# The first expert layer: routing by two tiles inside the last feed, experts in written order, fetched rows added tile by tile in the next layer

## The chip, the core and the metric

The kernel runs on one core of one Trainium2 chip. The metric is the device time of one execution, in microseconds (us), as the median of several runs. One core has five engines that work beside each other: TensorE (PE; its weight loads are listed apart as PEld), VectorE (DVE), ScalarE (ACT), GpSimd (POOL) and SyncE (SP). In this kernel SP issues nearly all DMAs, ACT some, and POOL those that take their row numbers from a tile (indirect DMAs: scatters and gathers).

## The reference, cut to what matters

The program is a stack of four layers of cross attention, self attention and feed-forward on 16 x 64 = 1024 tokens of width 256. The change touches the end of the first self-attention stage, the first feed-forward stage and the opening of the next cross attention.

The first self attention is a four-layer encoder with linear attention. Of each of its layers only the second half matters here, `x + relu(layernorm(x) @ W1 + b1) @ W2 + b2` with 1024 hidden features, and then a last layer norm, whose scaled result is added to the tokens. The expert layer after it is

```
logits = x @ gate_w.T
probs = softmax(logits)
top2_w, top2_idx = top_k(probs, 2)
cap = int(1.25 * T / E)                      # 160 of T = 1024, E = 8
counts = bincount(top2_idx.reshape(-1), length=E)
keep = (counts <= cap)
comb = zeros((T, E)).at[arange(T)[:, None], top2_idx].add(top2_w) * keep[None, :]
h = relu(einsum('th,ehf->tef', x, W1) + b1)
y = einsum('teh,ehf->tef', h, W2) + b2
out = einsum('te,tef->tf', comb, y)
```

so that an expert that more than 160 tokens choose gives nothing at all. In the program its output is added to the tokens. The next cross attention normalises the tokens, forms scores of the 64 slots of each of 16 groups against 1601 context rows, takes the softmax over the slots, and feeds weighted context sums to a recurrent cell (GRU), three times over.

## The kernel before, in words

**Tiles and stages.** The tokens lie in `self.x` as NT = 8 tiles of P = 128 tokens by D = 256 features (KC = 2 blocks of 128). `STAGES` (L2590) runs eleven stages one after the other, among them `l0_attn`, `l0_ffn` and `l1_xattn`. Where a stage sets `self.pinned`, TensorE takes its matmuls in the order in which they are written; engines wrapped in `Written` (L51, whose calls are all recorded as L59) keep their written order likewise. Elsewhere the scheduler orders.

**l0_attn** works on two halves, a and b, of HT = 4 tiles. Each half's work is written as generators, and `go(generator, n)` advances one by n steps, so the code writes out by hand how the halves take turns. The half-layer above is `feed` (L635): two steps that transpose the normalised tokens into hT (`turn`), eight steps c0 to c7 of one 128-feature group each (matmuls named lin_t, then a relu on ACT or DVE into h1T), four steps t0 to t3 of one tile each (matmuls named lin, added to y), and `finish` (L664) for each pair of tiles: the normalisation n and, in the last feed, its scale and the addition into x. `measure` takes a pair's mean and variance, `norm` makes n. In each step `squares` (L441) lets ACT do some of the squares of context rows ("junk" in the profile) which later stages need; the calls of one feed sum to 26.

After the layer loop comes, in this order (L822-L832): the rest of a's last feed; `squares(999)`, all squares left over, at once; b's last feed, into whose later steps the routing of a is put; the routing of b.

**Routing.** `route(s)` (L695) does four tiles at a time: normalise, transpose, 16 gate matmuls, then on DVE logits, a comparison of each expert's logit with each other's (rk_gt, rk_eq, of 4 x 8 x 8 columns), their sum rank, and sel (rank under 2). Two to five matmuls named pos count, for each token, how many tokens before it chose each expert; the count of half a is kept for half b. From pos come place, whether it fits within the 160 places, and two row numbers for each token: put, where its row is written, and get, where its result will be. Eight indirect DMAs on POOL (L758) scatter the rows of n into the DRAM buffer `taken`, which holds 160 places for each expert and spare rows behind.

**l0_ffn** (L850) loads `taken` back: xs holds the first 128 places of all experts (four DMAs), xw the last 32 (four DMAs, in groups of 32 partitions). All are transposed on TensorE into xsT. Then the softmax of the logits, and the weight wt of each token and choice. For each expert come the loads of W1 and W2 (SP's queue), eight matmuls (hidden), relu (hT), four matmuls (out), the bias into ys, and a DMA of ys into the DRAM buffer `given`; after every fourth expert 16 matmuls do the last 32 places of four experts, into yw and again into `given`. This stage isn't pinned. At its end (L941-L947) 16 indirect DMAs on POOL gather two rows for each token out of `given` into `got`, each followed by a DVE operation that multiplies by wt and adds to x.

**l1_xattn** (L950) loads keys (cT) and rows (cn) of two groups for each tile, and two small tiles raw and raw2 of GRU biases. `product(mqk)` multiplies two weights together, `first(tile)` normalises a tile into s, `queries` makes pq and qT. `biases` (L1012) splits raw into three bfloat16 parts by ten DVE operations on 32 partitions. `attend` makes scores (sc, TensorE), takes them off (ACT), transposes them (turn) and softmaxes over slots (DVE, POOL); `product(mvg)` multiplies two more weights; `update` sums context rows (pu, 52 matmuls) and runs the GRU. The order is that of L1270 onwards: mqk, first(tiles[0]), its queries, load_rows of tile 0, keys of tile 1, load_rows of tile 1, biases, attend, product(mvg), then the loop over tiles and iterations.

Of the kernel before, what the change touches and what calls it, by code (L numbers as in the profile page):

```python
# [20 lines left out]
P = 128  # L21
# [5 lines left out]
NCH = 13  # L27
# [37 lines left out]
class Sections:  # L65
# [343 lines left out]
    def l0_attn(self):  # L409
# [5 lines left out]
        self.route = to = Streamed(0)  # L415
        for name, shape, dt in (("logits", [P, NT, E], F32), ("count", [P, 2, E], F32), ("hot", [P, NT, 2, E], F32),
                                ("put", [P, NT, 2], I32), ("get", [P, NT, 2], I32)):
            setattr(to, name, pool.tile(shape, dt, tag=name, name=name))
# [12 lines left out]
            self.taken[: E * CAP].rearrange("(j p) d -> p j d", p=P), zero.unsqueeze(1).to_broadcast([P, E * CAP // P, D]))  # L431
        views = dram_disjoint_views(self.taken, 2 * NT)
        with ExitStack() as ctx:
# [201 lines left out]
            def feed(s, w, last=False):  # L635
# [15 lines left out]
                for t in range(HT):  # L651
                    pm = by_token(w.w2, t, s.h1T)
                    squares((4, 4, 4, 2)[t])
                    V.tensor_tensor(s.y[:, t, :], pm, s.y[:, t, :], ALU.add)
                    if t == 1:
                        measure(s, s.y, 0)
                    elif t == 2:
                        finish(s, 0, last)
                    yield
# [35 lines left out]
            def route(s):  # L695

                i = slice(s.i * HT, (s.i + 1) * HT)
                for p in range(2):
                    measure(s, s.x, p)
                for p in range(2):  # L700
                    norm(s, s.x, p)
                yield
                for p in range(2):
                    turn(s, p)
                    yield
                pm = ps.tile([P, HT, E], F32, tag="mm", name="gate", bufs=3, padded_shape=[P, 64, E])
                for t in range(HT):
                    for k in range(KC):
                        self.mm(pm[:, t, :], s.hT[:, k, t * P : (t + 1) * P], wg[:, k, :], start=(t == 0 and k == 0),
                                stop=(k == KC - 1), skip_group_check=True)  # L710
                own = to.logits[:, i]
                V.tensor_copy(own, pm)
                shape = [P, HT, E, E]
                other, each = own.unsqueeze(2).to_broadcast(shape), own.unsqueeze(3).to_broadcast(shape)
# [7 lines left out]
                rank = sb.tile([P, HT, E], F32, tag="rank", name="rank", bufs=2)  # L722
                V.tensor_reduce(rank, gt, AX.X, ALU.add)
                sel = sb.tile([P, HT, E], F32, tag="sel", name="sel", bufs=2)
                V.tensor_scalar(sel, rank, 1.5, 0.0, ALU.is_lt, ALU.add)
                yield

                pos = ps.tile([P, HT, E], F32, tag="mm", name="pos", bufs=3, padded_shape=[P, 64, E])
                self.mm(pos, prior, sel, start=True, stop=False, skip_group_check=True)
                for t in range(HT - 1):  # L730
                    n = HT - 1 - t
                    self.mm(pos[:, t + 1 :, :], self.c("ones"), sel[:, t : t + 1, :].to_broadcast([P, n, E]), start=False,
                            stop=(s.i == 0), skip_group_check=True)
                if s.i:
                    self.mm(pos, self.c("ones"), to.count[:, 0:1, :].to_broadcast([P, HT, E]), start=False, stop=True,
                            skip_group_check=True)
                V.tensor_reduce(to.count[:, s.i], sel.rearrange("p t e -> p e t"), AX.X, ALU.add)

                shape = [P, HT, 2, E]
                at = first.rearrange("p (t k e) -> p t k e", k=2, e=E)[:, i]  # L740
                by = pick.rearrange("p (k e) -> p k e", e=E).unsqueeze(1).to_broadcast(shape)
                V.tensor_tensor(to.hot[:, i], rank.unsqueeze(2).to_broadcast(shape), by, ALU.is_equal)
                place = sb.tile(shape, F32, tag="place", name="place", bufs=2)
                many = pos.unsqueeze(2).to_broadcast(shape)
                V.tensor_tensor(place, many, at, ALU.add)
                fits = sb.tile([P, HT, E], F32, tag="fits", name="fits", bufs=2)
                V.tensor_scalar(fits, pos, CAP - 0.5, 0.0, ALU.is_lt, ALU.add)
                V.tensor_tensor(to.hot[:, i], to.hot[:, i], fits.unsqueeze(2).to_broadcast(shape), ALU.mult)
                V.tensor_tensor(place, place, to.hot[:, i], ALU.mult)
                one = sb.tile([P, HT, 2], F32, tag="one", name="one", bufs=2)  # L750
# [4 lines left out]
                for t in range(HT):  # L755
                    for k in range(2):
                        j = 2 * (s.i * HT + t) + k
                        nc.gpsimd.indirect_dma_start(  # L758
                            views[j], bass.IndirectOffsetOnAxis(ap=to.put[:, s.i * HT + t, k : k + 1], axis=0),
                            s.n[:, t, :], None)  # L760
# [48 lines left out]
            for l in range(1, 4):  # L809
                w0, w = w, weights(l)  # L810
                for s, ws, o, wo in ((a, w, b, w0), (b, w, a, w)):
# [9 lines left out]
                    mix(at, fd)  # L821
            go(fd)  # L822
            squares(999)
            fd, rt = feed(b, w, True), route(a)
            go(fd, 4)
            go(rt, 1)
            go(fd, 2)
            for _ in range(4):
                go(rt, 1)
                go(fd, 1)  # L830
            go(fd)
            go(route(b))  # L832
# [17 lines left out]
    def l0_ffn(self):  # L850
# [3 lines left out]
        to = self.route  # L854
        with ExitStack() as ctx:
# [11 lines left out]
            got = sb.tile([P, NT, 2, D], F32, tag="got", name="got")  # L867
# [6 lines left out]

            for r in range(4):
# [5 lines left out]
            for r in range(4):  # L881
                nc.sync.dma_start(xw[W * r : W * (r + 1)], last(taken, r))

            def turn(src, j, to):
                pt = ps.tile([P, KC, 2, P], F32, tag="tr", name="tr")
                for c in range(KC):
                    for i in range(2):
                        nc.tensor.transpose(pt[:, c, i, :], src[:, j + i, c * P : (c + 1) * P], self.ident)
                for c in range(KC):
                    self.copy(to(c), pt[:, c])  # L890

            for e in range(0, E, 2):
                turn(xs, e, lambda c: xsT[:, c, e : e + 2, :P])
            pt = ps.tile([P, KC, 2, P], F32, tag="tr", name="tr")
            for c in range(KC):
                for i in range(2):
                    nc.tensor.transpose(pt[:, c, i, :], xw[:, i, c * P : (c + 1) * P], self.ident)
            for c in range(KC):
                self.copy(xsT[:, c, :, P:], pt[:, c].rearrange("p q (r s) -> p (q r) s", s=W))
# [3 lines left out]
            pc = ps.tile([P, E], F32, tag="tr", name="pc", padded_shape=[P, 512])  # L903
            for i in range(2):
                nc.tensor.matmul(pc, self.c("ones"), to.count[:, i, :], start=(i == 0), stop=(i == 1))
# [4 lines left out]
            wt = sb.tile([P, NT, 2], F32, tag="wt", name="wt")  # L910
            nc.vector.tensor_reduce(wt, to.hot, AX.X, ALU.add)

            hs = []
            for e in range(E):
                w1, w2 = self.w2(d["L0_ffn_W1"][e], "w1"), self.w2(d["L0_ffn_W2"][e], "w2")
                pm = ps.tile([P, KC, CAP], F32, tag="mm", name="hidden", padded_shape=[P, KC, 256])
                for n in range(KC):
                    for k in range(KC):
                        nc.tensor.matmul(pm[:, n, :], w1[:, k, n * P : (n + 1) * P], xsT[:, k, e, :],
                                         start=(n == 0 and k == 0), stop=(k == KC - 1), skip_group_check=True)  # L920
                hT = sb.tile([P, KC, CAP], F32, tag="hT", name="hT", bufs=6)
                for n in range(KC):
                    self.bias_relu(hT[:, n], pm[:, n], b1[:, 2 * e + n : 2 * e + n + 1])
                po = ps.tile([P, D], F32, tag="out", name="out", padded_shape=[P, 512])
                for k in range(KC):
                    nc.tensor.matmul(po, hT[:, k, :P], w2[:, k, :], start=(k == 0), stop=(k == KC - 1))
                nc.vector.tensor_tensor(ys[:, e], po, b2[:, e * D : (e + 1) * D], ALU.add)
                nc.sync.dma_start(given[:P, e], ys[:, e])
                hs.append((hT, w2))
                if e % 4 == 3:  # L930
                    q = e // 4
                    po = ps.tile([P, D], F32, tag="out", name="out", padded_shape=[P, 512])
                    for k in range(KC):
                        for r, (hT, w2) in enumerate(hs):
                            nc.tensor.matmul(po[W * r : W * (r + 1), :], hT[:, k, P:], w2[:, k, :], start=(k == 0),
                                             stop=(k == KC - 1))
# [1814 lines left out]
```

## Time and profile before

| | us |
|---|---|
| runs of the kernel, median of 3 (lowest to highest) | 3798.28 (3797.85 to 3800.1) |
| the profiled execution | 3790.97 |
| its span, first to last instruction | 3789.2 |
| TensorE busy in the span | 3440.1 |
| VectorE busy | 1965.6 |
| ACT busy | 1450.4 |
| POOL busy | 1290.4 |
| mean granted TensorE clock, as a share of full speed | 0.954 |

How to read it: the profile is one execution, so its durations are summed against its own 3790.97, not against the median of other runs. The stretch that the change touches lies between about 1282 and 1460 us of the span. A line of a timeline gives start, duration, engine, source line, operation, output and inputs, how many instructions it joins, and in brackets how long the engine sat idle before it and what released it. A line of the chain gives start, duration and what ran: following the chain back, each piece is what the next one waited for. Durations of neighbouring matmuls overlap, as they are pipelined.

### The profile page before, as it was taken

Reading aid. Unit: us, or ns where it says so; the run is one execution under the profiler, and the core shown is the slowest. Engines: PE = TensorE matmul, PEld = TensorE weight load, DVE = VectorE, ACT = ScalarE, POOL = GpSimd, SP = SyncE. Lnnn points to the kernel's source line nnn. Section 1 sums busy time; section 2 is a strip of 40 time slices with the busy share of each in tenths; the row PEclk is TensorE's granted clock in tenths of the full one; section 3 lists DMA queues with packets and bytes.
Section 4 is the critical chain, followed back from the end, with each engine's and each line's share of the span. In section 5 each row is a group of like instructions: output and inputs, shape, how many; then the busy total and the mean of one; then the engine's idle time right before and its main releaser. Section 6 shows DMA issues by size and latency. Waiting matters only on the chain.

```text
span 3789.2 us, 70696 instructions
## 1 busy us (share of the span) xinstructions
PE 3440.1 (91%) x30923; PEld 2179.8 (58%) x30938; DVE 1965.6 (52%) x3634; ACT 1450.4 (38%) x2072; POOL 1290.4 (34%) x788
## 2 busy tenths in 40 slices
PE   8999999996999848999977998999999789999986
PEld 4555555563666534555544666676767555555454
DVE  4334333335555435655656545576767655333346
ACT  2333333342444413444423433366666612111214
POOL 1555555561110122433421001577777630000012
PEclk9999999997999969999988999999999979999997
DMA  3111100102333344442101000211111004111650
GB/s 125 38 38 38 38 35 22 37 10 70 99 97 95 105 134 142 145 145 81 65 26 40 1 6 13 99 43 51 38 56 38 11 1 172 39 37 32 252 202 13
DMA packets 106045, 258.42 MB, mean 68 GB/s; under 512 B 9180, under 2 KB 74463, under 8 KB 103432
## 3 DMA queue, kind: packets, MB, share of 16 engines
q1 hardware_dynamic: 97288, 222.43, 16.6%
q10 hardware_dynamic: 6912, 27.27, 2.3%
q8 instruction: 243, 3.98, 0.4%
q0 software_dynamic: 1536, 4.20, 0.4%
q14 instruction: 66, 0.54, 0.0%
HBM read 248.10 MB, written 5.77 MB: 67 GB/s over the span
## 4 chain that ended last, share of the span: by engine, by line
PE 76%; DVE 12%; ACT 8%; issue 2%; POOL 1%; DMA 1%; SPq 0%; ACTq 0%; DVEq 0%; POOLq 0%
PE sc L2387 15%; PE pk L2387 15%; PE lin L2387 7%; PE acc L2387 6%; PE lin_t L2387 5%; ACT e L322 4%; PE pu L2387 4%; PE lin L194 3%; PE gate L1952 3%; PE up L1952 3%; PE pc L1574 3%; PE prz L2387 2%; PE gelu_t L1484 2%; PE turn L2392 2%; PE pn L2387 1%
## 5 line engine op out<-in xcount | busy, mean ns | idle before, releaser
L2320 POOL TENSOR_TENSOR tot<-tot,e 128x1024 f32<-128x1024 f32 (+1 forms) x340 | 803.1, 2362 | 374.2 <-ACT e L322 251.1
L265 DVE TENSOR_REDUCE m<-sc 128x4 f32<-128x2048 f32 x96 | 220.1, 2292 | 270.7 <-PE sc L2387 269.6
L1714 DVE SCALAR_TENSOR_TENSOR e<-sc,row_L_xattn_nbias,free 128x2048 f32<-128x2048 f32 x104 | 244.2, 2349 | 122.7 <-PE sc L2387 118.9
L1716 ACT ACTIVATE e<-e 128x2048 f32<-128x2048 f32 x104 | 198.7, 1910 | 243.1 <-DVE e L1714 243.1
L322 ACT ACTIVATE e<-sc 128x2048 f32<-128x2048 f32 x104 | 195.2, 1877 | 241.2 <-PE sc L2387 239.6
L2387 PE MATMUL sc<-qb,kT 32*128 32x128 f32 x6656 | 245.0, 283 | 36.3 <-DVE m L279 12.3
L2387 PEld LDWEIGHTS sc<-qb,kT 32*128 32x128 f32 x6656 | 206.1, 187 | 80.4 <-issue 24.5
L2387 PE MATMUL acc<-e,v 128*32 128x128 f32 x6656 | 226.3, 276 | 6.4 <-ACT e L1717 6.4
L2387 PEld LDWEIGHTS acc<-e,v 128*32 128x32 f32 x6656 | 170.0, 110 | 105.8 <-issue 95.2
L2387 PE MATMUL pk<-cT,wk 128*128 128x512 f32 (+1 forms) x512 | 206.4, 532 | 3.6 <-DVE rows L295 3.6
L2387 PE MATMUL pk<-wv,cT 128*128 128x256 f32 x832 | 208.6, 393 | 0.0
L1717 ACT ACTIVATE e<-e 128x2048 f32<-128x2048 f32 x104 | 198.7, 1911 | 3.3
L2387 PE MATMUL pk<-cT,wkv 128*128 128x512 f32 (+1 forms) x512 | 196.6, 524 | 0.0
L2387 PE MATMUL pk<-wkv,cT 128*128 128x256 f32 x832 | 196.3, 386 | 0.0
L2387 PEld LDWEIGHTS pk<-wv,cT 128*128 128x128 f32 x832 | 149.2, 189 | 75.3 <-issue 57.2
L2387 PEld LDWEIGHTS pk<-wkv,cT 128*128 128x128 f32 x832 | 153.2, 190 | 28.5 <-issue 4.3
L1574 PE MATMUL pc<-ew,eh 128*128 128x256 f32 x640 | 158.3, 390 | 0.0
L1119 POOL TENSOR_TENSOR e<-e,mx 128x512 f32<-128x512 f32 x96 | 81.6, 881 | 209.0 <-DVE mx L1118 209.0
L1956 ACT ACTIVATE g<-gate 128x512 f32<-128x512 f32 x68 | 40.6, 597 | 292.2 <-PE gate L1952 292.2
L2387 PE MATMUL sc<-kT,qb 32*128 32x512 f32 (+2 forms) x1536 | 140.2, 464 | 11.7 <-ACT e L322 0.7
L2387 PE MATMUL pu<-cn,e 128*64 128x257 f32 (+1 forms) x1248 | 143.5, 386 | 5.8 <-POOL e L1129 5.8
L2387 PE MATMUL sc<-cT,qT 128*64 128x512 f32 (+1 forms) x768 | 141.5, 521 | 0.5 <-DVE qT L1077 0.5
(524 smaller groups left out, 6228.1 us busy)
## 6 DMA issues: line engine op xcount, KB each, us to landing
cT<-in_ctx_t SPq DMA_DIRECT2D x128, 832.0 KB, 6.2
cn<-in_ctx_n SPq DMA_DIRECT2D x32, 1664.0 KB, 12.8
piece<-in_ctx_n ACTq DMA_DIRECT2D x32, 640.0 KB, 3.9
w<-in_L_attn_W SPq DMA_DIRECT2D x8, 1024.0 KB, 6.6
piece<-in_ctx_n ACTq DMA_DIRECT2D x16, 384.0 KB, 3.6
w<-in_L_ffn_W SPq DMA_DIRECT2D x16, 256.0 KB, 2.8
down<-in_L_ffn_w_down SPq DMA_DIRECT2D x16, 256.0 KB, 2.8
gate<-in_L_ffn_w_gate SPq DMA_DIRECT2D x16, 256.0 KB, 2.8
```

Source lines behind the costliest of these rows:

```text
L194: nc.tensor.matmul(pm, xT[:, k, t * P : (t + 1) * P], w[:, k, :], start=(k == 0), stop=(k == kc - 1))
L265: nc.vector.tensor_reduce(x.m4[:, g, :, i], pm, AX.X, ALU.max)
L322: nc.scalar.activation(e, pm, AF.Exp, scale=0.25)
L1119: pin(nc.gpsimd.tensor_tensor(p.e, p.e, p.mx.unsqueeze(2).to_broadcast(p.shape), ALU.subtract))
L1484: nc.tensor.matmul(pm, w[:, c, lo : lo + m], cT[:, c, :], start=(c == 0), stop=(c == nk - 1))
L1574: nc.tensor.matmul(pc[:, n, j, :], s.eh[i][:, c, tok], ew2[:, c, cols], start=False, stop=(c == 3))
L1714: nc.vector.scalar_tensor_tensor(e16, pm16, nb, free[:, at : at + P].unsqueeze(1).to_broadcast([P, 16, P]), ALU.add, ALU.mult)
L1716: nc.scalar.activation(e, e, AF.Relu)
L1717: nc.scalar.activation(e, e, AF.Square)
L1952: nc.tensor.matmul(pm[-1], w[:, k, n * P : (n + 1) * P], xT[:, k, tok], start=(k == 0), stop=(k == KC - 1))
L2320: nc.gpsimd.tensor_tensor(tot[:w], x.first if c == 1 else tot[:w], e[:w], ALU.add)
L2387: ins = self.nc.tensor.matmul(*args, **kw)
```

## The change

What it does, part by part:

- **Routing.** `route(s, p)` takes two tiles. The count of choices is kept as a running table of one row of eight for each tile, so that pos needs two matmuls: one of `prior` with sel, one of ones with two rows of the table. Gate matmuls, rank, sel and pos are one step.
- **Order at the end of l0_attn.** The two turns of b's last feed are issued before a's last finish; the routes of a stand between b's column groups c0 to c7; b's first pair is finished after its second tile (t1 where it was t2), and the routes of b follow the two pairs. `squares(999)` comes last, and 26 squares ride in b's feed.
- **Experts.** The weights of all experts are asked for ahead of the loads of `taken` (four experts in the shared weight buffers, four in tiles of the stage's own); xs of two experts and then xw are loaded first. The stage is pinned: hidden of an expert, the transposes for two later experts, then out of the expert before. The softmax and wt are written behind the experts.
- **Gathers.** `got` is made of two of the four cn buffers of l1_xattn. The 16 gathers and their additions move into l1_xattn: all gathers after product(mqk), product(mvg) and biases, which now come first; the additions tile by tile (`combine`), tile 0 before first(tiles[0]), the others further back.

The diff, cut to its core:

```diff
@@ l0_attn, feed
-                    elif t == 2:
+                    if t == (1 if last and s is b else 2):
                         finish(s, 0, last)
@@ route
-            def route(s):
+            def route(s, p):
...
+                count = to.count[:, 2 * g : 2 * g + 2]
+                V.tensor_tensor(to.count[:, 2 * g + 1], to.count[:, 2 * g], sel[:, 0], ALU.add)
+                pos = ps.tile([P, 2, E], F32, tag="mm", name="pos", bufs=3, padded_shape=[P, 64, E])
+                self.mm(pos, prior, sel, start=True, stop=False)
+                self.mm(pos, self.c("ones"), count, start=False, stop=True)
...
@@ end of l0_attn
+            fb = feed(b, w, True)
+            go(fb, 2)
             go(fd)
+            go(fb, 1)
+            for p in range(2):
+                measure(a, a.x, p)
+                rt = route(a, p)
+                go(fb, 1)
+                norm(a, a.x, p)
+                for _ in range(3):
+                    go(rt, 1)
+                    go(fb, 1)
+
+            go(fb, 2)
+            measure(b, b.x, 0)
+            go(fb, 1)
+            r0, r1 = route(b, 0), route(b, 1)
+            norm(b, b.x, 0)
+            go(r0, 1)
+            go(fb)
+            measure(b, b.x, 1)
+            norm(b, b.x, 1)
+            go(r0, 1)
+            go(r1, 1)
+            go(r0)
+            go(r1)
             squares(999)
-            fd, rt = feed(b, w, True), route(a)
-            go(fd, 4)
-            go(rt, 1)
-            go(fd, 2)
-            for _ in range(4):
-                go(rt, 1)
-                go(fd, 1)
-            go(fd)
-            go(route(b))
@@ l0_ffn
+            ws = [weights(e) for e in range(E)]
...
+            self.pinned = True
+            turn_two(0)
+            turn(xw, 0, lambda c, of: (xsT[:, c, :, P:], of.rearrange("p q (r s) -> p (q r) s", s=W)))
+            for e in range(E + 1):
+                if e < E:
+                    hidden(e)
+                    if e % 2 == 0 and e + 2 < E:
+                        turn_two(e + 2)
+                if e == 0:
+                    pc = ps.tile([P, E], F32, tag="tr", name="pc", padded_shape=[P, 512])
+                    self.mm(pc, self.c("ones"), to.count[:, NT], start=True, stop=True)
+                else:
+                    out(e - 1)
+                if e and e % 4 == 0:
+                    out_last(e // 4 - 1)
+            self.pinned = False
...
-            for t in range(NT):
-                for k in range(2):
-                    nc.gpsimd.indirect_dma_start(
-                        got[:, t, k, :], None, self.given, bass.IndirectOffsetOnAxis(ap=to.get[:, t, k : k + 1], axis=0))
-                for k in range(2):
-                    nc.vector.scalar_tensor_tensor(
-                        self.x[:, t, :], got[:, t, k, :], wt[:, t, k : k + 1], self.x[:, t, :], ALU.mult, ALU.add)
-        self.routed.close()
@@ l1_xattn
+            got = [sb2.tile([P, NCH, D + 1], F32, tag="cn", name="got", bufs=4) for _ in range(2)]
...
             product(mqk, wq, wk, w_s)
+            product(mvg, wv, wih, w_in)
+            biases()
+            for t in range(NT):
+                fetch(t)
+            combine(0)
             first(tiles[0])
...
             load_rows(tiles[0])
+            combine(1)
             keys(b[0])
+            combine(2)
+            combine(3)
+            attend(tiles[0], tiles[1])
+            for t in range(4, NT):
+                combine(t)
             load_rows(tiles[1])
-            biases()
-            attend(tiles[0], tiles[1])
-            product(mvg, wv, wih, w_in)
+            self.routed.close()
```

`fetch(t)` issues two indirect DMAs on POOL into `got`; `combine(t)` is the two DVE operations that were at the old place, kept in written order.

## The prediction, on record before the result

> **What bounds the kernel now.** I read the page's busy times first: TensorE works nine tenths of the span, so only stretches where it does not can be won.
>
> ```profile
> span 3789.2 us, 70696 instructions
> PE 3440.1 (91%) x30923; PEld 2179.8 (58%) x30938; DVE 1965.6 (52%) x3634; ACT 1450.4 (38%) x2072; POOL 1290.4 (34%) x788
> ```
>
> Then the table of stretches around the change (us, then busy PE, PEld, DVE, ACT, POOL, granted clock, DMA share, GB/s):
>
> ```profile
> 1284.00:1298.00 14.00, 2.07 (x2) 0.50 (x2) 3.87 (x8) 11.82 (x55) 0.65 (x1) 0.56 0.49 150
> 1298.00:1333.00 35.00, 33.38 (x126) 21.98 (x126) 15.81 (x51) 4.40 (x10) 7.93 (x8) 0.93 0.26 90
> 1333.00:1353.00 20.00, 7.88 (x34) 7.08 (x34) 12.33 (x47) 1.78 (x5) 0.17 (x1) 0.60 0.00 0
> 1353.00:1374.00 21.00, 5.91 (x25) 4.74 (x25) 4.69 (x13) 3.78 (x8) 8.54 (x9) 0.50 0.37 112
> 1374.00:1397.00 23.00, 20.86 (x130) 17.33 (x131) 7.47 (x22) 4.43 (x9) 0.00 (x0) 0.92 0.59 172
> 1402.00:1426.00 24.00, 0.00 (x0) 0.00 (x0) 7.39 (x16) 0.00 (x0) 15.44 (x16) 0.50 0.70 216
> ```
>
> TensorE is nearly idle in four stretches: ACT's (row 1), the routing chain (3), POOL's scatters (4), POOL's gathers (6). Between them feed and experts fill it. TensorE's timeline shows two ends of such waits:
>
> ```profile
> 1298.14 2.07 PE L2387 MATMUL lin_t<-hT,w 128*128 128x512 f32 x2 [7.77 <-ACT hT L59]
> ...
> 1428.43 0.69 PE L2392 MATMUL turn<-cst,s 128*128 128x128 f32 x2 [29.70 <-DVE s L2255]
> ```
>
> The chain says what ends last in each:
>
> ```profile
> 1290.18 1.31 ACT junk L59 x6
> ...
> 1319.13 13.83 PE lin L2387 x64
> ...
> 1361.75 2.42 DMA taken<-n,put
> ...
> 1365.76 5.18 DMA xs<-taken
> ...
> 1388.79 3.02 DMA w<-in_L_ffn_W
> ```
>
> So: junk squares ahead of ACT's hT copy; the lin matmuls; the last scatter's landing; the loads; late weights. The last views are VectorE's and SP's timelines where the next layer opens:
>
> ```profile
> 1433.61 1.21 DVE L1014 TENSOR_TENSOR raw<-raw 32x1024 f32<-32x1024 f32 x1 [1.45 <-DMA raw<-in_rows]
> ```
>
> ```profile
> 1403.00 24.07 SPq L972 DMA_DIRECT2D cT<-in_ctx_t  x4
> 1427.36 1.13 SPq L992 DMA_DIRECT2D raw<-in_rows  x3
> ```
>
> SP held two of four key loads for the adds (24 us), so raw was issued late; VectorE had it 6.2 us after issue.
>
> **The change part by part.** I keep marks: T, end of the last lin (1332.96); S, scatters landed (1364.17); E, end of the experts on TensorE (1396.9); s, first normalised tile (1428.4); F, end of the first pu group (1460.2).
>
> *Feed of b, to T.* TensorE's last transposes for a end at 1282.9, T is 50.1 later. Now b's turns stand ahead of a's finish and the 26 squares trail. hT follows VectorE's y (1282.5) by two copies, so lin_t starts at about 1283.65, not 1298.14. But finishing and routing now sit between column groups. From the changed order on each engine: groups c0 and c1 run to 1287.1; TensorE waits 3.3 while VectorE does a's second finish (n .73, scale .69, x .69), two measures, h1T .75, n .42; c2 and the first gate (half of 1.85) end at 1293.6; the two-tile rank chain stands in line (half-width, about .3 an operation where the four-tile row has .35-.43), 2.0; c3-c5 to 1301.1; wait 1.7; c6, gate, wait 2.0, pos to 1308.3; c7 1.72; lin 13.83; T'=1323.9. In sum 13.83+13.76+3.65 (transposes, gates, pos)+9.0 waiting after 1283.65. Gain 9.0. Before, route of a cost TensorE only one wait of 0.84: the waits are the price of no yield between gate and pos. The squares cost nothing: ACT's 11.8 us lie under lin; without that cover they would delay hT as before.
>
> A rule speaks against these waits. Rows: after 5.4 and 7.8 idle lin_t records take 853 ns, six of them, against 430; after 0.84 idle (ahead of pos at 1316.3) they stay at the fast time, as the experts' matmuls do after gaps of about 1.2 (1391.9). Nothing here shows 2.0 to 3.3. The Trainium skill, "TensorE: Matmul & The Clock Gate", section "HAM oscillation — how this bites in real kernels", says idle gaps over about 3.4 us drop TensorE to half rate. By the rows the sum stands; by the rule 3.3 is at the edge, and one drop costs some 2-3 us (six records times .42). I take none, as three waits of four are nearer to the fast rows, and keep 0 to 5 for the range.
>
> *T to S.* Before 31.2: n, 8 transposes, gate x16 3.48 on a cold TensorE, rank chain 2.7, pos, place, then 8 scatters at a 1.26 pitch and 2.42 landing. Now r0 starts when b's first pair is finished (t1): VectorE finish and measure to T+7.7, logits and rank to T+9.5, pos T+10.6, place T+12.3, 4 scatters to T+17.4; r1 follows under them (gate T+14.2, sel +16, pos +17, place +18.65), its 4 scatters 4x1.26, landing included T+25.0. Gain 6.2: about four scatters (5.0) and narrower chains. S'=1348.9.
>
> *S to first hidden.* Before 9.8: four xs, four xw issues (.47 each), 5.18 for xs, transposes. Now xs0 and xw go first (five issues 2.4, landing 2.7, 8 transposes and copies): 6.0. Gain 3.8. Softmax leaves its old place, on VectorE behind the experts' copies, ahead of E'+5.
>
> *Experts.* Before 22.9; the chain has 3.02 for a late weight, which loading ahead removes; three transpose groups (.6 each) and the pc move in. 22.5. E'=1377.4, a gain of 19.5 there. SP's wk, wv and the given writes stand behind the same matmuls as before; the weight loads now end well ahead of xs.
>
> *E to s.* Before 31.5: yw writes, first gather at E+5.3, sixteen at 1.26, landing 4.43, adds, LN. Now tile 0 needs only two gathers. But VectorE runs, in order: mqk, mvg (to E'+7.6), the biases, combine(0), LN. The biases' first add waits for raw. SP issues wo, wq, wo (.79 MB), four cT (3.4 MB; nothing holds them now, got is elsewhere), then raw at E'+6.5 to 7.6. Before, raw landed when 1.7 MB of cT ahead had: 5.5 us moving, about 305 GB/s; with gathers running the trace moved 389-422 GB/s, of which gathers are some 105. 4.2 MB at 300 take 14: raw lands at E'+19.3. Biases 10.6 (1.21+3x(.68+1.20+1.27)), combine .96, LN 1.65: s'=E'+32.6. Loss 1.1: the gathers' freed 20 us turn into waiting for raw. If raw landed as an unhindered transfer does (2.42 in the last scatter's row), at E'+10, s would be at about E'+23, ten earlier; each us later costs one.
>
> Here too a rule is against: "DMA: Bandwidth & Descriptors", section "Queues, rings and completion order", says that each DMA engine consumes the descriptors of one issuing engine in ring order, which lets the 18 KB of raw wait out the megabytes ahead of them on SP's ring, now twice as many. The row bears that out behind two cT (6.2 us); by row and rule E'+19.3, by the free landing E'+10. I take the former.
>
> *s to F.* Before 31.8, with biases (ten operations on VectorE between scale and weights) and the mvg product (11 us of TensorE's 1444.8-1456) inside. Both are now in front, in TensorE's idle time; added are combines 1-7, 14 x .48 = 6.7, part under sc (32 matmuls, 7.8). I take 28.8, a gain of 3.0; bounds 0 and 6. F'=1377.4+32.6+28.8=1438.8: 21.4 earlier than 1460.2. The second tile's cn loads wait for combine(3) and (7), since got has two of four cn buffers: about E'+56, landing (12.8) E'+69; pu of tile 1 is some 14 later, so hidden; without that cover a us per us. Past it the order on all engines is the old one.
>
> **The rivals.**
> *Raw lands early.* Small packets slip in between rings: s'=E'+23, gain 31, 3767. For: all 16 DMA engines share it, nothing held. Against: the row of before. 0.15.
>
> *Waits in the feed eat it.* Stalls longer and cold, the route tail bound by VectorE's order: 5 for clock, 4 longer waits, 2 in the tail; gain 10, 3788. For: VectorE has every new chain. 0.14.
>
> *Slower: raw held far behind.* One mechanism: the biases stand in VectorE's queue before combine(0), and raw behind four cT on SP's ring while the gathers take the DMA engines. It decides when raw lands 21.4 later than E'+19.3, i.e. SP's 4.2 MB take 35 us (118 GB/s) from E'+5; at 90 GB/s they take 47, raw lands 33 later than in the sum, and the time is 3776.9+33=3810. Against: 389-422 GB/s moved in 1405-1413 with gathers on. 0.05.
>
> *It does not do what it says:* the head start of first layers is lost to a wait that hides gathers anyway. That is in the sum as E to s; only if everything from T to E' is lost as well is the time the same, 3798. 0.06.
>
> **How the numbers follow.** 9.0+6.2+3.8+0.4−1.1+3.0=21.3, from marks 21.4. The profiled run took 3790.97, 1.77 outside its span; it would take 3769.6, its span 3767.8. It lies 7.3 under the median of the runs shown; with the same offset the median is 3776.9, put as 3777. A measurement tells about 0.2%, 7.6 us, from no change: faster means under 3790.7. Main case 0.60, 3770 to 3784. Faster: .60+.15+.13 of the feed rival = .88; same: .06 and the feed rival's last .01 = .07; slower .05. Range 3764 (raw early, with the feed at its best) to 3788 (the feed eats half); what is left out is the tails beyond these, the no-change and the slower case, under 0.2 together.
>
> **What would show it.** Right: lin_t of b from about 1284; last lin near 1324; four scatters after the last pos; S' to hidden about 6; no w wait in the experts; a VectorE wait of about 11 us on raw before the biases, s some 32 after E'. Wrong: lin_t records of 853 ns after the waits; raw landed within 10 of E'; TensorE waiting for cn in tile 1; a stretch later than the first pu that changed its length.

## The result, and the profile after

Five runs of the changed kernel have a median of 3779.26 us (3775.53 to 3781.53), beside 3798.28 for five of the kernel before (3788.5 to 3804.06). The ratio is 0.995, with a 95% interval of 0.9933 to 0.9967: 19 us less, and by the interval 12.5 to 25. The profiled execution took 3775.53 with a span of 3773.7; that of before took 3790.97 with 3789.2.

A single median of this program moves by more than the parts of the change are worth. So I read the marks of the prediction out of each trace, counted from the end of a's last transposes on TensorE (1282.90 before, 1284.94 after). Three marks are taken where the next work starts: S at SP's first load of `taken`, s at the first transposes of the next layer, F at the first prz matmul.

| us | before | after | gain | forecast gain |
|---|---|---|---|---|
| a's last transposes to T, b's last lin | 50.05 | 46.21 | 3.8 | 9.0 |
| T to S, scatters landed | 31.36 | 25.39 | 6.0 | 6.2 |
| S to first hidden | 9.65 | 5.78 | 3.9 | 3.8 |
| experts, to E | 22.85 | 21.34 | 1.5 | 0.4 |
| E to s | 31.62 | 34.76 | -3.1 | -1.1 |
| s to F | 31.92 | 29.21 | 2.7 | 3.0 |
| sum | 177.45 | 162.69 | 14.8 | 21.3 |

From a's last transposes to the end of the span the changed kernel is 17.5 shorter; 2.8 of it lies behind F, where the order of instructions is the old one. In the kernels below, which have the old order there too, this rest took between 2323.5 and 2337.1 (2328.9 before, 2326.1 after), so I put it to no part of the change.

The page's first lines show no new load, only less idle time: busy sums moved by under 7 us on every engine.

```profile
span 3773.7 us, 70724 instructions
PE 3435.9 (91%) x30919; PEld 2176.2 (58%) x30934; DVE 1972.4 (52%) x3672; ACT 1450.6 (38%) x2072; POOL 1291.7 (34%) x789
```

The table of stretches of the changed kernel (columns as before: us, busy PE, PEld, DVE, ACT, POOL, granted clock, DMA share, GB/s):

```profile
1286.00:1298.00 12.00, 7.23 (x28) 3.94 (x27) 7.76 (x28) 5.00 (x18) 0.71 (x1) 0.98 0.20 46
1298.00:1333.00 35.00, 30.44 (x106) 20.48 (x105) 16.44 (x62) 10.76 (x46) 7.93 (x8) 0.86 0.57 195
1333.00:1347.00 14.00, 4.97 (x25) 4.31 (x24) 9.81 (x41) 1.58 (x4) 2.82 (x3) 0.58 0.05 19
1347.00:1362.00 15.00, 3.21 (x12) 2.36 (x12) 5.45 (x24) 2.29 (x4) 7.68 (x9) 0.50 0.38 124
1362.00:1384.00 22.00, 21.68 (x144) 19.00 (x145) 9.49 (x26) 5.92 (x13) 0.00 (x0) 0.91 0.31 96
1392.00:1405.00 13.00, 0.00 (x0) 0.00 (x0) 0.02 (x1) 0.00 (x0) 9.65 (x12) 0.55 1.02 371
```

Row 1 is no longer empty, rows 3 and 4 are shorter than theirs were. Row 2 has a granted clock of 0.86 with 30.4 of 35 us busy: TensorE is working at half rate in the middle of the feed. In row 6 TensorE and ACT do nothing for 13 us and VectorE next to nothing, while POOL issues gathers and the DMA engines are full. TensorE's timeline shows the inside of the feed:

```profile
1292.08 0.78 PE L2434 MATMUL tr<-cst,n 128*128 128x128 f32 x4 [2.79 <-DVE n L59]
1292.70 1.88 PE L2429 MATMUL lin_t<-hT,w 128*128 128x512 f32 x4
1294.41 0.95 PE L2429 MATMUL gate<-wg,hT 128*128 128x8 f32 x8
1297.35 0.40 PE L2429 MATMUL pos<-sel,places 128*128 128x16 f32 x2 [1.98 <-DVE sel L59]
1297.64 0.58 PE L2429 MATMUL pos<-count,cst 128*128 128x16 f32 x2
1298.06 6.87 PE L2429 MATMUL lin_t<-hT,w 128*128 128x512 f32 x12
...
1311.83 0.61 PE L2429 MATMUL pos<-sel,places 128*128 128x16 f32 x2 [1.98 <-DVE sel L59]
1312.28 0.59 PE L2429 MATMUL pos<-count,cst 128*128 128x16 f32 x2
1312.71 3.76 PE L2429 MATMUL lin_t<-hT,w 128*128 128x512 f32 x4
1316.26 14.89 PE L2429 MATMUL lin<-w,h1T 128*128 128x256 f32 x64
```

The four records of one column group (c2) take 1.88. The twelve of c3 to c5 take 6.87, where three groups at the full rate would take about 5.4. The four of c7 take 3.76, and lin 14.89 where it took 13.98. And VectorE's and SP's timelines show what fills row 6:

```profile
1404.98 1.22 DVE L1049 TENSOR_TENSOR raw<-raw 32x1024 f32<-32x1024 f32 x1 [13.46 <-DMA raw<-in_rows]
```

```profile
1387.97 2.21 SPq L989 DMA_DIRECT2D cT<-in_ctx_t  x4
1390.29 1.25 SPq L1025 DMA_DIRECT2D raw<-in_rows  x3
```

SP holds nothing any more (24.07 for the four cT before), yet raw is ready only 13.4 us after its last load was issued.

### The profile page after: what moved, and what is told of

It is laid out like the page before. It is cut to its first block, busy times and chain, and to the rows that moved or that the text cites. A ratio compares the mean times of both kernels' runs of the same rounds, so it can differ in the third digit from the quotient of the medians.

```text
span 3773.7 us, 70724 instructions
## 1 busy us (share of the span) xinstructions
PE 3435.9 (91%) x30919; PEld 2176.2 (58%) x30934; DVE 1972.4 (52%) x3672; ACT 1450.6 (38%) x2072; POOL 1291.7 (34%) x789
## 4 chain that ended last, share of the span: by engine, by line
PE 77%; DVE 12%; ACT 7%; issue 3%; POOL 0%; DMA 0%; ACTq 0%; SPq 0%; DVEq 0%; POOLq 0%
PE sc L2429 15%; PE pk L2429 15%; PE lin L2429 7%; PE acc L2429 6%; PE lin_t L2429 5%; ACT e L322 4%; PE pu L2429 4%; PE lin L194 3%; PE gate L1994 3%; PE up L1994 3%; PE pc L1616 3%; PE prz L2429 2%; PE gelu_t L1526 2%; PE turn L2434 2%; PE pn L2429 1%
```

## The experiments

In all of them the marks are read as above; medians stand beside runs of the kernel before on the same chip. The three kernels with filled waits were executed once each, and only their traces are read.

**The two waits in the feed: move the wait, or fill it.** My theory was that the waits for sel cost themselves and the half clock behind them. The rival: VectorE's order bounds the stretch wherever pos stands. The first run puts a step between sel and pos.

```diff
                 V.tensor_scalar(sel, rank, 1.5, 0.0, ALU.is_lt, ALU.add)
+                yield
...
-                for _ in range(3):
+                for _ in range(4):
                     go(rt, 1)
                     go(fb, 1)
-            go(fb, 2)
             measure(b, b.x, 0)
...
-            go(r0, 1)
+            go(r0, 2)
             go(r1, 1)
```

> The changed kernel with one step more in the routing: a yield between sel and the pos matmuls, so that a column group (or a lin tile) of b's feed stands on TensorE between the gate and pos. All is computed. In the changed kernel's trace TensorE waits 1.98 us twice for sel, and the lin_t records behind run partly at 853 ns (c3-c5 took 6.87 us where 5.16 is warm, c7 3.76 where 1.72 is). Theory: the stalls cost themselves and the half clock behind them, so the stretch from a's last transposes to b's last lin (46.2 us) falls to 38-40, 6 to 8 us less, and the median falls by as much (about 3772). Rival: the stretch is bound by VectorE's order, not by the position of pos; then the wait only moves to the next transposes or the next group, and the stretch stays within 2 us of 46.

Median 3771.93 beside 3789.72, ratio 0.9947 (0.9929 to 0.9964). The stretch to T took 38.60, 7.6 less than the changed kernel's, and F came 8.9 earlier: the theory's number, and the rival falls. The waits of this stretch, behind the first 0.65, sum to 5.25 here and to 8.30 in the changed kernel, so some 3 of the 7.6 are waiting and the rest is clock. That is what the change paid for having gate matmuls, rank, sel and pos in one step. By its ratio, though, this kernel can't be told from the changed one (0.995, 0.9933 to 0.9967), and the same holds for the two below that bring raw or the biases into a better place: what these three gain over the changed kernel stands in the traces alone.

The next three keep the order and put idle matmuls into the stalls, to part the clock from the wait: four in each in the first, two in each in the others.

```diff
-                pos = ps.tile([P, 2, E], F32, tag="mm", name="pos", bufs=3, padded_shape=[P, 64, E])
+                pos = ps.tile([P, 64, E], F32, tag="mm", name="pos", bufs=3)
+                if s is a:
+                    for _ in range(4):
+                        self.mm(pos.rearrange("p t e -> p (t e)"), w.w1[:, 0, :P], b.hT[:, 0, :], start=True, stop=True)
+                pos = pos[:, :2]
                 self.mm(pos, prior, sel, start=True, stop=False)
```

> The changed kernel with four idle matmuls (128x512, as lin_t) put into the place of each of the two 1.98 us stalls of a's routes; their result is overwritten by pos. All is computed. If the half clock behind the stalls comes from the idle time, the lin_t of c3-c5 take 5.2 us again (6.87 now) and those of c7 1.72 (3.76 now), and the stretch from a's last transposes to b's last lin falls from 46.2 to 42-43 though the order is the same and work is added. If the slow records have another cause (weights or PSUM), the stretch stays at 46 or grows.

The stretch fell only to 45.57, by less than the 3 expected at least: I had counted four matmuls as four records, and each is two, so that the filling took 3.68 in a wait of 1.98; and c2, behind the 2.79 wait, took 3.15 where it took 1.88. But behind the filling the lin_t of c3 to c5 took 5.40, c7 1.96 and lin 13.98. Right on the clock, wrong on the sum.

> As the run with four idle matmuls in each of the two stalls for sel, which overran them (3.68 us in a stall of 1.98), with two in each: 1.7 us, inside the stall. All is computed. If the half clock comes from the idle time, c3-c5 take 5.4 and c7 1.96 as with four, lin 13.98, and the stretch from a's last transposes to b's last lin falls from 46.2-47.8 to 41.5-43.5. If it only came from having more work, it stays at 45 or more.

The stretch took 43.08. What is left of the half clock stands ahead of the filled waits: this one's c2, behind the 2.79 wait, took 3.20. The last run fills that wait too, with three matmuls into a tile of their own ahead of the first route's transposes.

> As the run with two idle matmuls in each stall for sel, and three more ahead of the first route's transposes, inside the 2.79 us stall there. All is computed. If it is the 2.79 us stall that starts the drop and the others follow, this one shows no lin_t record at 853 ns at all and the stretch is 41.5 or under. If the stalls for sel alone start it, it is the same as with two in each, within 1 us.

The stretch took 41.46, and no record is slow any more. Its timeline on TensorE, at the same places:

```profile
1289.13 0.78 PE L2442 MATMUL tr<-cst,n 128*128 128x128 f32 x4 [0.22 <-DVE n L59]
1289.75 1.88 PE L2437 MATMUL lin_t<-hT,w 128*128 128x512 f32 x4
...
1294.40 0.39 PE L2437 MATMUL pos<-sel,places 128*128 128x16 f32 x2 [0.16 <-DVE sel L59]
...
1294.90 5.40 PE L2437 MATMUL lin_t<-hT,w 128*128 128x512 f32 x12
...
1307.67 1.96 PE L2437 MATMUL lin_t<-hT,w 128*128 128x512 f32 x4
1309.47 13.98 PE L2437 MATMUL lin<-w,h1T 128*128 128x256 f32 x64
```

So in the changed kernel's trace the clock alone cost 46.21-41.46=4.75; the waits stayed as they were, only filled.

Which wait brings the half clock on isn't settled by this run alone. Behind the same 2.79 wait, unfilled, c2 took 1.88 in five traces and 3.15 to 3.24 in five others, two of them the filled runs above. The granted clock tells them apart. In each of the twelve traces all its changes lie whole multiples of 3.41 us apart, and where these marks fall against the work differs from trace to trace. These are stretches from mark to mark, columns as in the table, first in the changed kernel, then in the run with raw first below, whose feed is the same:

```profile
1287.39:1290.80 3.41, 1.90 (x5) 0.57 (x3) 3.24 (x10) 1.08 (x3) 0.00 (x0) 1.00 0.41 115
1290.80:1294.22 3.42, 2.14 (x8) 1.29 (x9) 1.42 (x4) 1.58 (x6) 0.00 (x0) 1.00 0.00 0
1294.22:1297.63 3.41, 1.43 (x11) 1.14 (x10) 2.02 (x10) 1.99 (x7) 0.00 (x0) 1.00 0.21 29
1297.63:1301.04 3.41, 3.41 (x8) 1.86 (x8) 0.07 (x1) 0.00 (x0) 0.00 (x0) 0.50 0.44 166
```

```profile
1289.91:1293.33 3.42, 0.64 (x3) 0.17 (x2) 3.20 (x10) 1.00 (x5) 0.00 (x0) 1.00 0.28 102
1293.33:1296.74 3.41, 3.41 (x8) 1.86 (x8) 0.00 (x0) 0.58 (x1) 0.00 (x0) 0.50 0.00 0
```

```profile
1294.00 3.24 PE L2429 MATMUL lin_t<-hT,w 128*128 128x512 f32 x4
```

In the changed kernel the 2.79 wait is shared by two stretches (1.51 and 1.28 idle) and the clock stays; the wait of 1.98 lies whole in the third, and the next is at half rate. In the other the whole 2.78 lies in one stretch, and c2 pays for it. So it is in all ten traces: c2 was slow in the five where the wait lay whole in one stretch, and fast in the five where it was shared. The changed kernel's feed therefore cost 46.2 to T in three traces and 47.7 to 47.8 in three others. How much idle time in a stretch is enough stays open: 1.98 was here, 1.99 was not in the kernel before (from 1446.10).

**The wait for raw.** Theory: raw waits out the bytes ahead of it on SP's ring, and the biases hand that on to s, one for one. Rival: the wait hides gathers and keys that would be waited for anyway. Two runs move raw's loads, one ahead of the keys' loads (SP's order became three weights, one cT, raw), one behind the two cn loads.

```diff
-            load_keys(tiles[0])
-
             at = ROWS_AT["L1_xattn_gru_bih"][0], ROWS_AT["L1_xattn_gru_bhh"][0]
             raw, raw2 = (sb2.tile([32, 4 * D], F32, tag="e", name="raw", padded_shape=[32, NCH * P]) for _ in range(2))
...
             for t, to, of, n in ((raw, 0, at[0], G), (raw, G, at[1] + 2 * D, D), (raw2, 0, at[1], 2 * D)):
                 nc.sync.dma_start(t[24:27, to : to + n], d["rows"][:, of : of + n].to_broadcast([3, n]))
+            load_keys(tiles[0])
+
```

> The changed kernel with the raw loads written ahead of the keys' loads; SP's order becomes three weights, one cT, raw, three cT. All is computed. Theory: raw waits out the bytes ahead of it on SP's ring; now 1.6 MB instead of 4.2, so it lands about 11 us after the experts' end (E) where it took 21.3, and s comes at E+24 instead of E+34.7; pu then waits for cn, so the end of the first pu gains 8 to 11; median about 3769. Rival: the biases' wait only hides the gathers and the keys; then s gains but sc waits for cT or pu for cn, and the end of pu gains under 3 us.

```diff
-            for t, to, of, n in ((raw, 0, at[0], G), (raw, G, at[1] + 2 * D, D), (raw2, 0, at[1], 2 * D)):
-                nc.sync.dma_start(t[24:27, to : to + n], d["rows"][:, of : of + n].to_broadcast([3, n]))
...
+            load_rows(tiles[0])
+            for t, to, of, n in ((raw, 0, at[0], G), (raw, G, at[1] + 2 * D, D), (raw2, 0, at[1], 2 * D)):
+                nc.sync.dma_start(t[24:27, to : to + n], d["rows"][:, of : of + n].to_broadcast([3, n]))
             product(mqk, wq, wk, w_s)
...
             take_queries(tiles[0])
-            load_rows(tiles[0])
```

> The changed kernel with raw's loads written behind the two cn loads of tile 0, so that SP's ring holds 7.6 MB ahead of raw where it held 4.2. All is computed. This is the forecast's slower rival turned up: if the biases ahead of combine(0) pass raw's landing on to s one for one, raw lands some 12 us later (3.3 MB more at about 280 GB/s), about E+33, and s comes at E+46 or so. The end of the first pu follows by 8 to 12, a little less because cn comes earlier; median within 0.2% of 3790. If raw's landing is not what holds s, s stays near E+34.

VectorE's timeline of the run with raw first, and of the one with raw last, at the same instruction:

```profile
1398.28 1.21 DVE L1049 TENSOR_TENSOR raw<-raw 32x1024 f32<-32x1024 f32 x1 [4.25 <-DMA raw<-in_rows]
```

```profile
1418.81 1.21 DVE L1047 TENSOR_TENSOR raw<-raw 32x1024 f32<-32x1024 f32 x1 [27.42 <-DMA raw<-in_rows]
```

| bytes ahead of raw on SP's ring, weights included | raw used at | s at | F at (us after E) |
|---|---|---|---|
| 1.6 MB (raw first) | 12.11 | 25.51 | 54.85 |
| 4.2 MB (changed kernel) | 21.32 | 34.76 | 63.97 |
| 7.6 MB (raw last) | 35.28 | 48.69 | 77.79 |

s follows raw by 13.4 in all three, and F follows s by 29.1 to 29.3: the theory holds at both ends. Two sizes were missed: with raw last F came 13.8 later where 8 to 12 were expected, and with raw first the first pu didn't wait for cn but, as in the changed kernel, for POOL's e (7.36). With raw last the whole gain is gone: F comes 177.83 after a's last transposes (177.45 before), the median is 3789.66 beside 3792.98, ratio 0.9996 (0.9984 to 1.0009). With raw first the median was 3771.63, ratio 0.9943 (0.9927 to 0.996).

The next run leaves raw's loads and moves the biases back behind combine(3).

> The changed kernel with the biases back behind combine(3), ahead of attend, raw's loads where they were. All is computed. Theory (VectorE's order, biases ahead of combine(0), costs the wait): s at E+14 to 15 (first gather at E+5.3, landed some 6 later, combine, LN) instead of E+34.7; the scores then wait for cT, landing with raw at about E+20; biases stand between scale and weights; end of first pu 9 to 13 earlier. Rival (the DMA volume bounds): the end of pu moves under 4 us, as cT and cn come when they come.

s came 15.95 after E, F 10.6 earlier than in the changed kernel (53.35 after E); median 3769.28, ratio 0.9939 (0.9921 to 0.9958). The gathers' head start was there all the time; VectorE's order hid it.

**Parts of the change alone.** l0_attn of the changed kernel with the rest of before:

> One part of the change alone: l0_attn of the changed kernel (routing by two tiles, new order of b's feed, squares last), with the expert stage and the next layer of the kernel before (pc from the running table). All is computed. By the marks this part gives 3.8 to b's last lin and 6.0 from there to the landed scatters: the stretch from a's last transposes to the first load of taken is 71.6 to 73.2 (81.4 before), everything behind as before, so about 9 less, 3781 to 3790 by its median. Rival: the gain is given back behind, as the experts meet weights that are not there yet; then the stretch to the experts' end gains less than 6.

Median 3778.97 beside 3792.98, ratio 0.996 (0.9945 to 0.9976). To S it took 71.66 and to F 165.47, 12.0 less than before: 9.8 to S and 2.0 in the experts, which I had not expected. The trace shows where the 2.0 come from: the first 14 hidden matmuls took 2.17 where they took 4.04 in the kernel before, whose clock was at half until 1377.83, 3.9 after hidden began; here it was full from 1363.05, just ahead of hidden. The 12.0 are four fifths of the whole at F. Then the pinned experts as well, with the gathers where they were:

> Two parts of the change: l0_attn and the pinned experts of the changed kernel, with gathers and additions at their old place at the end of the expert stage, and the next layer of the kernel before. All is computed. Theory: the experts part is worth 5.4 (3.9 from the reordered loads, 1.5 in the experts), and moving the gathers is worth nothing to s and about nothing to the end of the first pu (64.0 against 63.5 after the experts' end). Then this kernel equals the changed one within 3 us. Rival: the move of the gathers carries the gain, and this one lies 6 or more above the changed kernel.

Median 3778.45, ratio 0.9959 (0.9943 to 0.9975). E came 3.3 earlier than with the first part alone, and F not at all (165.46). What was won was given back: 1.3 to s, of which 0.91 is a wait of VectorE for ACT's part of the layer norm (ln_r) that the first part alone doesn't have, and 2.0 from s to F. Of these, 1.0 lies in the scores (sc took 7.76 where the first part alone took 6.76) and 1.0 in the mvg product with its waits (11.87 where it took 10.85). Both are clock. The product's second half shows once more that the length of a wait does not decide; first in this run, then in the kernel before:

```profile
1434.78 5.49 PE L2413 MATMUL pw<-wih,wv 128*128 128x512 f32 x8 [3.71 <-DVE mvg L1061]
```

```profile
1451.24 2.85 PE L2387 MATMUL pw<-wih,wv 128*128 128x512 f32 x8 [3.72 <-DVE mvg L1035]
```

Here 2.39 of the wait fell into one stretch between the clock's marks, there no more than 1.99.

The changed kernel lies 2.8 below this one at F, as "within 3" had it. But 2.0 of that are the clock just named, and from E to F the changed kernel took 63.97, the first part alone 63.44 and the kernel before 63.54. That the third part, gathers, biases and mvg product together, is worth anything is not shown.

**Both waits gone.** The step in the routing, and the biases behind the first tile's weights, for which raw and raw2 share one buffer:

```diff
+            both = sb2.tile([32, NCH * P], F32, tag="e", name="raw")
+            raw, raw2 = both[:, : 4 * D], both[:, 4 * D : 6 * D]
...
             product(mvg, wv, wih, w_in)
-            biases()
...
                 x.exp()
                 x.weigh()
+            biases()
```

> The changed kernel with the routing's yield, and with the biases written behind the first tile's weights; for that raw and raw2 share one buffer of tag e. All is computed. Theory: both waits the runs showed go at once, TensorE's in the feed (7.6 less) and VectorE's for raw (10.6 less with the biases ahead of attend, some 5 more with the biases out of the way of scale): end of first pu 18 to 25 earlier than in the changed kernel, median about 3755. Rival: with s early, the scores wait for cT and pu for cn, and the end of the first pu gains no more than with the biases merely late (18).

Median 3754.52 (3751.37 to 3758.31) beside 3792.98, ratio 0.9892 (0.9873 to 0.9911): faster than both kernels, for its interval lies clear of the changed kernel's. F came 142.72 after a's last transposes, 20.0 less than in the changed kernel. Its TensorE timeline shows what stands there next:

```profile
1414.58 5.02 PE L2429 MATMUL pu<-cn,e 128*64 128x257 f32 x32 [7.37 <-POOL e L1162]
1419.77 2.40 PE L2429 MATMUL pu<-cn,e 128*64 128x257 f32 x20 [0.17 <-POOL e L1162]
1427.75 0.59 PE L2429 MATMUL prz<-bias,three 128*128 128x512 bf16 x1 [5.58 <-DVE bias L1055]
```

The biases are now late for prz, by 5.58. Against the run with biases merely late, E to F fell by only 2.4 (50.98 against 53.35): of the two parts of my expectation the first came, and of the "some 5 more" half. Neither cT nor cn is waited for.

## Why the prediction was right, point by point

The time was forecast as 3777 and came at 3779.3. The mechanisms were those forecast, with three sizes off; that the median came so near is in part luck, as the last paragraph says.

- **Feed of b.** Order and waits were as forecast: lin_t from 0.65 after the transposes, waits of 2.79, 1.98, 1.55 and 1.98 where 3.3, 2.0, 1.7 and 2.0 stood. The step that failed is "I take none" for the clock: by the filled stalls it cost 4.75, nearly the whole gap between 9.0 and 3.8, and at the far end of the 0 to 5 that I kept for the range. I had weighed the waits by their length against rows with other waits. What counted was how much of a wait falls into one of the stretches of 3.41 us between which the clock changed, and a whole wait of 1.98 was enough. The rule of the Trainium skill ("TensorE: Matmul & The Clock Gate", section "HAM oscillation — how this bites in real kernels", gaps over about 3.4 us) would have let each of them pass, for none is longer than 2.79. Here the measurement decides against reading it gap by gap, in both directions: in the kernel before the clock stayed up behind a wait of 3.72.
- **T to S, and S to hidden** were right within 0.3: 6.0 and 3.9. The last scatters are four instead of eight, and xs0 and xw are enough to start.
- **Experts** gained 1.5 instead of 0.4; no wait for a weight is left. The 3.02 that I read as the cost of a late weight is the time of that DMA on the chain; TensorE's own waits for weights were 0.42 and 1.17 before. Why the stage came out shorter by more than forecast is otherwise not shown.
- **E to s.** The mechanism was right: the gathers' freed time turned into VectorE's wait for raw. The term "4.2 MB at 300" was too fast: raw came at 21.3, not 19.3, so about 257 GB/s for SP's ring from E+5 on. The sentence that I followed from the Trainium skill, "DMA: Bandwidth & Descriptors", section "Queues, rings and completion order", is borne out by three points, 1.6, 4.2 and 7.6 MB.
- **s to F** gained 2.7 of 3.0; pu itself ran at the half clock behind its 7.36 of waiting (8.55 instead of 5.87), and the time ahead of it was shorter than I had it. cn for the second tile wasn't waited for.
- **The rivals.** The feed's rival, 5 for the clock, is in the result, but without the longer waits and the tail it named. Raw early didn't happen; the run that made it happen gained 9.1, near the ten forecast. The slower rival was no fancy: raw behind 7.6 MB ate the gain, though its 14 us are short of the 21 that it had as its turning point, because the gain was smaller.

At F the sum was 6.5 too high (21.3 against 14.8). The median hides that by luck: 2.8 came behind F, from no part of the change, and the changed kernel's profile lay only 3.7 below its median, where that of before lay 7.3 below. The profiled execution itself was forecast at 3769.6 and took 3775.53.

## What to carry to other kernels

When work is put between another engine's steps, leave a step between the producer's matmul and the consumer's, or the other engine's chain comes out as a wait; here one yield was worth 7.6 us of the stretch. Moving a slow transfer out of an engine's way helps only if what then stands first in that engine's queue is ready: see what its first operation waits for, and where that small load stands on its ring. And where TensorE waits for some 2 us or more, read the granted clock behind the wait in more than one trace: the same wait of 2.79 was free in five traces here and brought half rate on in five.

## What the runs showed of the hardware that was not expected

TensorE's granted clock changed only at marks whole multiples of 3.41 us apart, in all twelve traces, and where the marks fell decided whether the same feed took 46.2 or 47.8 to T. A wait of 1.98 us was enough to bring half rate on, and the half rate was gone when the waits were filled with idle matmuls. A wait of 3.72 us, shared by two stretches, left the clock up.
